# Mixing the filter matrices behind the second image's first chunk

## The chip, the cores and the metric

The kernel runs on one core of one Trainium2 chip. The metric is the device time of one execution in microseconds (us), the median of the runs shown. All data is float32.

## What is computed

Two images of 128 channels and 64 x 64 points go through two layers. The first layer is a group norm, a windowed attention (7 x 7 neighbours, 4 heads) and a small row of linear layers. The second layer treats each image as 4096 tokens of 128 channels:

```python
t = _to_tokens(x)
t = t + _L1_attn_ref(_ln_t(t))          # softmax(q q^T / sqrt(128), diagonal masked) q
t = t + _L1_ffn_ref(_ln_t(t), sigma, phi, M_u, M_phi_plus, M_phi_minus, log_weights, gumbel)
```

The "ffn" is a causal convolution of the tokens with 16 long filters `phi`, each followed by a 128 x 128 matrix, and three short lags with matrices of their own:

```python
out = jnp.einsum('btkd,k,kde->bte', U_plus, s, Mpp)          # s = sigma ** 0.25
out = out + jnp.einsum('btkd,k,kde->bte', U_minus, s, Mpm)
```

There are four such branches, over the whole, the half, the quarter and the eighth of the sequence. They are summed with weights from `log_weights + gumbel`. The kernel uses that the sum over the branches can be taken over the matrices: for each of the 16 filters it mixes the four branches' `M_phi_plus` and `M_phi_minus` by the weights, takes sum and difference, and scales by `s`. This mixing is what the change moves.

## The kernel before, in words

The work runs in this order. First the windowed attention of both images, band by band, in an order that a table of due times (`PLAN`) sets. Then the global attention of image 0 (`attention(0, fill)`, L1233), that of image 1 (L1268), and last the convolution (L1288 and below), where TensorE multiplies spectra (L1320) and applies the mixed matrices (L1332).

`attention` (L882) cuts the 4096 tokens into 8 chunks of 512 and walks over the 36 pairs of chunks. For each pair TensorE makes four score tiles (L899), ScalarE takes their exponentials (L906), and TensorE applies them in both directions: straight (`other`, L952) and, after a transpose (L913) that VectorE copies out of PSUM with a row sum (L916), onto `own` (L927). Pairs on the diagonal have no transposes; on them VectorE adds to the diagonal (L904). The pairs go (0,0), (0,1) ... (0,7), (1,1) ..., so that a chunk is complete at the end of its row.

Between these steps `attention` calls `fill()`. A call asks generators for one more piece of side work each. `filler` (L1191) keeps two lists: `urgent`, which holds one `after` generator (L969) for each finished chunk, and `steps`. Each call goes first to `urgent`, then to `steps`; a generator that yields `None` ends the call, one that yields `True` passes it to the next list. `after` turns a finished chunk back into tokens (L976, L981), takes their layernorm into a tile `z` (L986, L987: statistics L174 and L175, the power on GpSimd L165, the application L182), transposes `z` (L193), transforms it (L1012, L1022) and stores the spectra (L1001, L1030).

Before the change, image 1's `steps` are what image 0 left over (its last `after` generators and the short lags, L1043 to L1060), then `filter_matrices` (L1121), then `load_blocks` (L1259). `filter_matrices` calls `mixed` (L1109), which loads 256 KB at a time into a tile `st` with two buffers (L1114) and sums the four branches on VectorE (L1117, L1119); then come the sum, the difference and the scaling (L1130 to L1135). It fills `mpl` and `mmi`. `load_blocks` fetches the first four blocks of filter spectra `ct` by DMA (L1254). The table `inv` is loaded (L1285) and scaled on VectorE (L1287).

These tiles have no place of their own. The pool `first` holds image 0's normalised tokens `tok[0]` and their transposed copy `cm[0]` (L134, L135), 16 KB each per partition. It is closed at L1237, after image 0's attention is written down, and `mpl`, `mmi`, `inv` and the blocks take its place. So the first write into them has to wait until the last reader of that place is done.

Outside the first attention the order on each engine isn't written by hand: a scheduler orders the instructions at build time by the order in which they were written, the dependencies and its own estimates of durations, and may bring forward one that is free to go. [...] All DMAs named here are issued from SyncE's (SP's) queue.

Of the kernel before, what the change touches and what calls it, by code (L numbers as in the profile page):

```python
# [8 lines left out]
F32 = mybir.dt.float32  # L9
AF = mybir.ActivationFunctionType  # L10
ALU = mybir.AluOpType
# [3 lines left out]
P = 128  # L15
# [6 lines left out]
KF = 16  # L22
# [60 lines left out]
CB, FB, SG = 256, 8, 4  # L83
# [12 lines left out]
def kernel(  # L96
# [16 lines left out]
    nc = tc.nc  # L113
# [4 lines left out]
    first_ = ExitStack()  # L118
# [9 lines left out]
    for c in range(4):  # L128
# [3 lines left out]
    tt, tok, cm = [None, None], [None, None], [None, None]  # L132
# [17 lines left out]
        out=flip, in_=flip, compare_op=ALU.not_equal, fill=1.0, base=1 - QT * QT, pattern=[[0, 2], [1, QT * QT]],  # L150
# [8 lines left out]
    seg = const.tile([P, NBR], F32, name="seg")  # L159
# [26 lines left out]
    def layernorm(dst, src):  # L186

        ln_apply(dst, src, ln_statistics(src))

    def transposed(ps, src):  # L190

        for j in range(src.shape[1]):
            nc.tensor.transpose(ps[:, j * P : (j + 1) * P], src[:, j, :], ident)  # L193
# [30 lines left out]
    with l0a:  # L224
# [6 lines left out]
        sp = l0a.enter_context(tc.tile_pool(name="l0_s", bufs=2))  # L231
# [27 lines left out]
        def table(ci, h, eng):  # L259
# [16 lines left out]
            out=gavg, in_=gavg, compare_op=ALU.is_ge, fill=0.0, base=0,  # L276
# [3 lines left out]
            out=gavg, in_=gavg, compare_op=ALU.is_ge, fill=0.0, base=3,  # L280
# [571 lines left out]
    t_in, t_filter, t_out = _transforms()  # L852
# [5 lines left out]
    with ap_:  # L858
        tp = ap_.enter_context(tc.tile_pool(name="l1_t", bufs=1, side="right"))
        ep = ap_.enter_context(tc.tile_pool(name="l1_e", bufs=8, side="right"))  # L860
        sp = ap_.enter_context(tc.tile_pool(name="l1_s", bufs=2, side="right"))
# [3 lines left out]
        def bank():  # L865
            return ps_m.tile([P, 512], F32, tag="bank", name="bank")
# [15 lines left out]
        def attention(b, fill):  # L882
# [55 lines left out]
            for i, (a, c) in enumerate(pairs):  # L938
# [27 lines left out]
                        nc.vector.tensor_copy(xs, other)  # L966
                es = coming

        def after(b, c, part):  # L969

            n0 = 4 * c
            ph, f0 = divmod(n0, FB)
            par, h = divmod(ph, 2)
            pt = bank()
            for j in range(4):
                nc.tensor.transpose(pt[:, j * P : (j + 1) * P], xa[b][:, (n0 + j) * P : (n0 + j + 1) * P], ident)  # L976
            rden = sp.tile([P, 4], F32, tag="rden", name="rden")
            nc.vector.tensor_reduce(rden, part[:, n0 : n0 + 4, :], AX.X, ALU.add)
            nc.vector.reciprocal(rden, rden)
            for j in range(4):  # L980
                nc.vector.scalar_tensor_tensor(  # L981
                    tt[b][:, n0 + j, :], pt[:, j * P : (j + 1) * P], rden[:, j : j + 1], tt[b][:, n0 + j, :],
                    ALU.mult, ALU.add,
                )
            yield
            z = sp.tile([P, 4, P], F32, tag="z4", name="z4")  # L986
            layernorm(z, tt[b][:, n0 : n0 + 4, :])  # L987
            yield
            yield True
            pt = bank()  # L990
            transposed(pt, z)
            s0 = 1 + h * (TH // 2)
            nc.scalar.copy(
                zc[:, par, s0 : s0 + TH // 2].rearrange("p (c f) -> p f c", f=FB)[:, f0 : f0 + 4, :],
                pt.rearrange("p (f c) -> p f c", f=4),
            )
            yield
            z2 = z.rearrange("p f d -> p (f d)")

            def store(m0, q, src):  # L1000
                nc.sync.dma_start(  # L1001
                    out=us[m0 // 2 : (m0 + P) // 2, :, 2 * h + q, f0 : f0 + 4, b, par, :].rearrange(
                        "g r f d -> (g r) f d"
                    ),
                    in_=src.rearrange("p (f d) -> p f d", d=P),
                )

            for m0 in (0, P):
                for q in range(2):
                    rows_ = slice(q * SB, (q + 1) * SB)  # L1010
                    pu = bank()
                    nc.tensor.matmul(pu, lhsT=tr[rows_, h, m0 : m0 + P], rhs=z2[rows_], start=True, stop=True)  # L1012
                    ub = sp.tile([P, 512], F32, tag="ub", name="ub", bufs=3)
                    (nc.scalar.copy if q else nc.vector.tensor_copy)(ub, pu)
                    store(m0, q, ub)
                yield

            banks = [bank() for q in range(2)]
            for i in range(2):
                for q in range(2):  # L1020
                    rows_ = slice(q * SB, (q + 1) * SB)
                    nc.tensor.matmul(  # L1022
                        banks[q][i * 64 : (i + 1) * 64, 0:256], lhsT=tr[rows_, h, 2 * P : NC],
                        rhs=z2[rows_, i * 256 : (i + 1) * 256], start=True, stop=True,
                    )
            ub = sp.tile([P, 512], F32, tag="ub", name="ub", bufs=3)
            for q in range(2):
                (nc.scalar.copy if q else nc.vector.tensor_copy)(ub[:, q * 256 : (q + 1) * 256], banks[q][:, 0:256])
                for i in range(2):
                    nc.sync.dma_start(  # L1030
                        out=us[P:, :, 2 * h + q, f0 + 2 * i : f0 + 2 * i + 2, b, par, :].rearrange("g r f d -> (g r) f d"),
                        in_=ub[i * 64 : (i + 1) * 64, q * 256 : (q + 1) * 256].rearrange("p (f d) -> p f d", d=P),
                    )
            yield

        def short_lags(b, h):

# [83 lines left out]
        def filter_matrices(mpl, mmi):  # L1121

            for k0 in range(0, KF, 4):
                for dst, src in ((mpl, m_plus), (mmi, m_minus)):
                    mixed(dst[:, k0 : k0 + 4, :], src[:, k0 : k0 + 4])
                    yield

                a, d = (m[:, k0 : k0 + 4, :].rearrange("p k e -> p (k e)") for m in (mpl, mmi))
                s = sp.tile([P, 512], F32, tag="st", name="mdiff")
                nc.vector.tensor_tensor(s, a, d, ALU.subtract)  # L1130
                nc.vector.tensor_tensor(a, a, d, ALU.add)
                for k in range(4):
                    ks = slice(k * P, (k + 1) * P)
                    nc.vector.tensor_scalar(a[:, ks], a[:, ks], sg[:, k0 + k : k0 + k + 1], None, ALU.mult)
                    nc.vector.tensor_scalar(d[:, ks], s[:, ks], sg[:, k0 + k : k0 + k + 1], None, ALU.mult)  # L1135
                yield
# [94 lines left out]
        steps = [drain(), chosen, filters(), tokens(1, bank)]  # L1231
        fill, left = filler(0, steps)
        attention(0, fill)  # L1233
        for gen in steps:
            for _ in gen:
                pass
        first_.close()  # L1237
        l1 = ctx.enter_context(tc.tile_pool(name="l1", bufs=1))
        mpl = l1.tile([P, KF, P], F32, name="mpl")
        mmi = l1.tile([P, KF, P], F32, name="mmi")  # L1240
        inv = l1.tile([P, 3, CB], F32, name="inv")
        ctp = ctx.enter_context(tc.tile_pool(name="blocks", bufs=5))

        def blocks(q):

# [13 lines left out]
        def load_blocks():  # L1259
            for q in range(4):  # L1260
                first_blocks.append(blocks(q))
                yield

        steps = [*left, filter_matrices(mpl, mmi), load_blocks()]

        kept = []
        fill, left = filler(1, steps, kept)
# [13 lines left out]

    tb_ = nc.inline_tensor(t_out, "t_out").ap().rearrange("(a p) c -> p a c", p=P)
    nc.sync.dma_start(out=inv, in_=tb_)  # L1285
    for s, (lo, hi) in enumerate(((0, 32), (32, 64), (64, 128), (128, 256))):
        nc.vector.tensor_scalar(inv[:, :, lo:hi], inv[:, :, lo:hi], seg[:, s : s + 1], None, ALU.mult)  # L1287
    outf = out.rearrange("b c h w -> b c (h w)")  # L1288
    with ExitStack() as cv:
        cp = cv.enter_context(tc.tile_pool(name="conv", bufs=5))  # L1290
# [142 lines left out]
def _transforms():  # L1433


    import numpy as np

    f = np.arange(BINS)[None, :]
    real = (f == 0)

    def parts(n):
        n = np.arange(n)[:, None]
        a = 2 * np.pi * ((f * n) % NC) / NC
        return np.cos(a), -np.sin(a), (1.0 - 2.0 * (n % 2)) + 0.0 * f

    def pack(*cols):
        return np.stack(cols, axis=-1).reshape(cols[0].shape[0], -1).astype(np.float32)

    c, m, alt = parts(CB)
    seg = pack(c, np.where(real, alt, m))  # L1450
    filters = pack(c, np.where(real, 0.0, m), np.where(real, 0.0, -m), np.where(real, alt, c))
    back = np.zeros((3 * P, CB), np.float32)

    back[0:NC] = pack(np.where(real, 1.0, 2.0 * c) / NC, np.where(real, alt, 2.0 * m) / NC).T
    back[NC:] = back[2 * P : NC]
    return seg, filters, back
# [51 lines left out]
```

## Time and profile before

| | us |
|---|---|
| median of 3 runs | 2209.53 (2209.5 to 2211.03) |
| the profiled execution's own time | 2211.93 |
| its span, first to last instruction | 2210.2 |
| TensorE busy (98% of the span) | 2156.2 |
| VectorE busy (42%) | 938.0 |
| ScalarE busy (35%) | 780.6 |
| image 1's attention begins (first score tiles) | 816.9 |
| image 1's first chunk is complete (its L976) | 944.7 |
| image 1's second chunk is complete (its L976) | 1028.2 |

A line of the profile names the engine, the line of the kernel, the operation, the written and read tiles and their shapes. "x2" is the number of instructions in a merged row. A bracket at the end, as in `[1.60 <-DVE z L182]`, says how long the engine had been idle before the row and which instruction released it. PE is TensorE, PEld its weight loads, DVE is VectorE, ACT is ScalarE, POOL is GpSimd, SPq is SyncE's queue, where DMAs are issued.

### The profile page before, as it was taken

The numbers are of one execution on the slowest core, as the hardware profiler recorded it, in microseconds if no ns is written. First come the engines' busy times: TensorE is split into PE (matmuls) and PEld (weight loads), VectorE is DVE, ScalarE is ACT, GpSimd is POOL, SyncE is SP. The second block draws the span as 40 slices with busy tenths as digits, with TensorE's granted clock in tenths as the row PEclk, the third lists the DMA queues.
The fourth block names the chain that finished last, engine by engine and source line by source line (L and its number), as shares of the span: only waits on it lengthen the run. The fifth ranks groups of instructions, "written<-read, shape, count | busy, mean of one in ns | idle before, by whom it ended". The sixth has DMA issues, their size and how long they took to land.

```text
span 2210.2 us, 31763 instructions
## 1 busy us (share of the span) xinstructions
PE 2156.2 (98%) x11920; PEld 1335.0 (60%) x11920; DVE 938.0 (42%) x3054; ACT 780.6 (35%) x1904; POOL 278.5 (13%) x355
## 2 busy tenths in 40 slices
PE   7899998999999998999999999999999999999998
PEld 4677765544554444544544447767767676777776
DVE  5899985434443346433333442232222323232232
ACT  3898883222333222222223232232222323232232
POOL 3477874200000000000000000000000000000000
PEclk8999999999999999999999999999999999999999
DMA  4222212021000025000000141221212121212101
GB/s 147 61 62 61 62 50 52 0 77 43 24 24 25 24 68 156 24 25 24 0 25 24 48 111 40 59 52 47 59 44 55 43 56 43 57 42 57 40 10 77
DMA packets 170345, 110.54 MB, mean 50 GB/s; under 512 B 21311, under 2 KB 155087, under 8 KB 169680
## 3 DMA queue, kind: packets, MB, share of 16 engines
q1 hardware_dynamic: 169266, 105.01, 17.8%
q8 instruction: 94, 1.54, 0.3%
q0 software_dynamic: 576, 2.10, 0.3%
q10 hardware_dynamic: 350, 1.41, 0.3%
q14 instruction: 59, 0.48, 0.1%
HBM read 73.86 MB, written 34.63 MB: 49 GB/s over the span
## 4 chain that ended last, share of the span: by engine, by line
PE 88%; DVE 5%; POOL 3%; DMA 2%; ACT 1%; issue 1%; SPq 1%; POOLq 0%; DVEq 0%; ACTq 0%
PE acc L1332 25%; PE pc L1320 13%; PE own L927 11%; PE bank L899 11%; PE other L952 8%; PE bank L913 4%; PE bank L333 2%; PE bank L1053 2%; PE bank L193 1%; PE bank L543 1%; PE bank L1012 1%; PE py L1354 1%; PE bank L507 1%; DMA st<-in_m_minus_dram 1%; PE po L565 1%; DVE ln_st L379 1%
## 5 line engine op out<-in xcount | busy, mean ns | idle before, releaser
L1321 DVE COPY y<-pc 128x512 f32<-128x512 f32 x320 | 221.6, 692 | 351.5 <-PE pc L1320 347.8
L906 ACT ACTIVATE e<-bank 128x512 f32<-128x512 f32 x288 | 171.8, 597 | 516.2 <-PE bank L899 387.8
L899 PE MATMUL bank<-cm 128*128 128x512 f32 x576 | 297.9, 601 | 1.4 <-DVE y L654 1.4
L1332 PE MATMUL acc<-y,mpl 128*128 128x256 f32 x1280 | 292.1, 382 | 0.0
L1332 PE MATMUL acc<-y,mmi 128*128 128x256 f32 x1280 | 288.0, 379 | 0.0
L1320 PE MATMUL pc<-ct,ut 64*128 64x512 f32 x1280 | 285.2, 595 | 0.9 <-issue 0.9
L1332 PEld LDWEIGHTS acc<-y,mpl 128*128 128x128 f32 x1280 | 238.1, 190 | 59.4 <-issue 29.6
L1332 PEld LDWEIGHTS acc<-y,mmi 128*128 128x128 f32 x1280 | 242.6, 190 | 32.6
L927 PE MATMUL own<-et,tok 128*128 128x512 f32 x448 | 228.5, 597 | 7.5 <-DVE part L916 7.4
L1321 ACT COPY y<-pc 128x512 f32<-128x512 f32 x320 | 205.1, 641 | 86.6 <-PE pc L1320 86.6
L952 PE MATMUL other<-e,tok 128*128 128x512 f32 x448 | 229.7, 594 | 0.0
L1320 PEld LDWEIGHTS pc<-ct,ut 64*128 64x128 f32 x1280 | 121.5, 187 | 145.8 <-issue 140.6
L916 DVE CUSTOM_DVE_ANT_0 et<-bank,one 128x512 f32<-128x512 f32 x224 | 145.5, 687 | 131.5 <-PE bank L913 131.4
L1339 ACT COPY ob<-acc 128x256 f32<-128x256 f32 x32 | 19.0, 595 | 387.0 <-PE acc L1332 387.0
L927 PEld LDWEIGHTS own<-et,tok 128*128 128x128 f32 x448 | 84.4, 191 | 117.5 <-issue 73.3
L952 PEld LDWEIGHTS other<-e,tok 128*128 128x128 f32 x448 | 85.2, 191 | 107.8 <-issue 106.0
L1356 DVE TENSOR_TENSOR xa<-py,xa 128x512 f32<-128x512 f32 x32 | 22.1, 692 | 281.4 <-PE py L1354 281.4
L913 PEld LDWEIGHTS bank<-ident,e 128*128 128x128 f32 x896 | 102.9, 141 | 55.4 <-issue 47.0
L899 PEld LDWEIGHTS bank<-cm 128*128 128x128 f32 x576 | 94.5, 191 | 67.9 <-issue 44.7
L165 POOL TENSOR_TENSOR ln_rs<-ln_rs,mhalf 128x4 f32<-128x4 f32 x24 | 24.5, 1020 | 837.1 <-DVE ln_rs L164 837.1
L530 ACT ACTIVATE p<-p,mn 128x196 f32<-128x196 f32 x256 | 114.4, 449 | 14.3 <-DVE mn L520 13.8
L913 PE MATMUL bank<-ident,e 128*128 128x128 f32 x896 | 117.2, 274 | 0.0
(210 smaller groups left out, 2289.3 us busy)
## 6 DMA issues: line engine op xcount, KB each, us to landing
ut<-us SPq DMA_DIRECT2D x80, 256.0 KB
us<-ub SPq DMA_DIRECT2D x64, 256.0 KB
vw<-vd SPq DMA_DIRECT2D x256, 49.0 KB
ct<-gs SPq DMA_DIRECT2D x160, 72.0 KB
ct<-gs SPq DMA_DIRECT2D x160, 64.0 KB
gs<-sum SPq DMA_DIRECT2D x20, 256.0 KB
vd<-v SPq DMA_DIRECT2D x128, 32.0 KB
st<-in_m_plus_dram SPq DMA_DIRECT2D x16, 256.0 KB
```

The lines of the kernel that those rows point to most:

```text
L333: nc.tensor.matmul(pl, lhsT=wg[:, lo : lo + P], rhs=zT, start=True, stop=True)
L530: nc.scalar.activation(p, p, AF.Exp, bias=t[name + "mn"][:, h : h + 1], scale=-1.0, accum_out=t["den"][:, u, h : h + 1],)
L899: nc.tensor.matmul(ps, lhsT=cm[b][:, n * P : (n + 1) * P], rhs=cm[b][:, chunk(c)], start=True, stop=True)
L906: nc.scalar.activation(e, ps, AF.Exp, bias=0.0, scale=ASCALE, accum_out=part[:, n, c : c + 1])
L913: nc.tensor.transpose(pt[:, k * P : (k + 1) * P], es[k][:, m * P : (m + 1) * P], ident)
L916: nc.vector.tensor_tensor_reduce(et, pt, one, 1.0, 0.0, ALU.mult, ALU.add, part[:, n, a : a + 1])
L927: nc.tensor.matmul(own, lhsT=tok[b][:, n, :], rhs=e, start=first, stop=last)
L952: nc.tensor.matmul(other, lhsT=tok[b][:, 4 * CHUNKS[a] + j, :], rhs=es[j], start=(j == 0), stop=(j == 3))
L1053: nc.tensor.matmul(py, lhsT=mu[:, lag, :], rhs=zc[:, from_par, s0 : s0 + 512], start=(lag == 0), stop=(lag == 2))
L1320: nc.tensor.matmul(pc, lhsT=ut[fp, b, par, :], rhs=cv_[fp], start=True, stop=True)
L1321: (nc.scalar.copy if f else nc.vector.tensor_copy)(y[:, 4 * f : 4 * f + 4, :, par, b * 2 * FB + q : (b + 1) * 2 * FB : 2], pc.rearrange("p ...
L1332: nc.tensor.matmul(acc, lhsT=(mmi if l else mpl)[:, k, :], rhs=y[:, 1::2, k, ::-1, :] if l else y[:, 0::2, k, :, :], start=(l == 0 and k = ...
```

## The change

`filter_matrices`, the load and scaling of `inv` and `load_blocks` become one generator, `for_ffn`. It stands where the two generators stood in image 1's `steps`. As long as a flag isn't set it yields `True` and does nothing. The flag is the list `spare`: it starts with a slice of image 0's token tile, `tok[0][:, 0:4, :]`. The first `after` of image 1 takes that slice as its `z` in place of a tile of its own, and when it is at its end it puts `None` into the list. Only then does `for_ffn` close the pool `first`, open the pools behind it and begin the mixing. No instruction of the mixing is added or removed.

```diff
+        spare = [tok[0][:, 0:4, :]]
+
         def after(b, c, part):
...
-            z = sp.tile([P, 4, P], F32, tag="z4", name="z4")
+            borrowed = b == 1 and spare not in ([], [None])
+            z = spare.pop() if borrowed else sp.tile([P, 4, P], F32, tag="z4", name="z4")
             layernorm(z, tt[b][:, n0 : n0 + 4, :])
...
             yield
+
+            if borrowed:
+                spare.append(None)
...
-        first_.close()
-        l1 = ctx.enter_context(tc.tile_pool(name="l1", bufs=1))
-        mpl = l1.tile([P, KF, P], F32, name="mpl")
-        mmi = l1.tile([P, KF, P], F32, name="mmi")
-        inv = l1.tile([P, 3, CB], F32, name="inv")
-        ctp = ctx.enter_context(tc.tile_pool(name="blocks", bufs=5))
+        mpl, mmi, inv, ctp = [None] * 4
...
-        steps = [*left, filter_matrices(mpl, mmi), load_blocks()]
+        def for_ffn():
+
+            nonlocal mpl, mmi, inv, ctp
+            while spare != [None]:
+                yield True
+            first_.close()
+            l1 = ctx.enter_context(tc.tile_pool(name="l1", bufs=1))
+            mpl = l1.tile([P, KF, P], F32, name="mpl")
+            mmi = l1.tile([P, KF, P], F32, name="mmi")
+            inv = l1.tile([P, 3, CB], F32, name="inv")
+            ctp = ctx.enter_context(tc.tile_pool(name="blocks", bufs=5))
+            yield from filter_matrices(mpl, mmi)
+
+            nc.sync.dma_start(out=inv, in_=nc.inline_tensor(t_out, "t_out").ap().rearrange("(a p) c -> p a c", p=P))
+            for s, (lo, hi) in enumerate(((0, 32), (32, 64), (64, 128), (128, 256))):
+                nc.vector.tensor_scalar(inv[:, :, lo:hi], inv[:, :, lo:hi], seg[:, s : s + 1], None, ALU.mult)
+            yield
+            yield from load_blocks()
+
+        steps = [*left, for_ffn()]
...
-    tb_ = nc.inline_tensor(t_out, "t_out").ap().rearrange("(a p) c -> p a c", p=P)
-    nc.sync.dma_start(out=inv, in_=tb_)
-    for s, (lo, hi) in enumerate(((0, 32), (32, 64), (64, 128), (128, 256))):
-        nc.vector.tensor_scalar(inv[:, :, lo:hi], inv[:, :, lo:hi], seg[:, s : s + 1], None, ALU.mult)
```

## The prediction

> **What bounds the kernel now.** I read the page's engine line first, then TensorE's (PE's) waits by stretches of 200 us, then the table of stretches around the only place where PE waits for work of the change, and last the orders of PE and VectorE (DVE) in it. The page and the waits of PE from 800 to 1300 us (us in total, times, longest):
>
> ```profile
> PE 2156.2 (98%) x11920; PEld 1335.0 (60%) x11920; DVE 938.0 (42%) x3054; ACT 780.6 (35%) x1904; POOL 278.5 (13%) x355
> PE own L927 <- DVE part L916: 6.5, 5, 4.4
> PE bank L193 <- DVE z L182: 5.1, 3, 1.9
> PE own L927 <- DVE xa L931: 1.6, 2, 0.8
> ```
>
> PE is the bound nearly everywhere. A change that adds and removes no matmul can only win or lose PE's idle time and its slow clock. Both sit in one place. The table (stretch, its length, busy us of PE, PEld, DVE, ACT, POOL; granted clock; DMA share; GB/s):
>
> ```profile
> 816.00:830.00 14.00, 13.19 (x42) 5.19 (x43) 7.30 (x16) 6.62 (x18) 0.28 (x1) 1.00 0.72 194
> 830.00:850.00 20.00, 15.58 (x44) 7.13 (x42) 13.94 (x44) 4.63 (x12) 1.30 (x1) 0.83 0.60 165
> 850.00:900.00 50.00, 48.46 (x167) 23.45 (x166) 34.67 (x82) 11.47 (x29) 0.00 (x0) 1.00 0.44 127
> 900.00:940.00 40.00, 40.00 (x134) 20.55 (x133) 12.06 (x34) 8.95 (x26) 0.00 (x0) 1.00 0.00 0
> 980.00:1020.00 40.00, 40.00 (x136) 20.76 (x136) 12.38 (x36) 8.95 (x26) 0.00 (x0) 1.00 0.00 1
> ```
>
> The second image's attention starts at 816. The mixing (L1117 to L1135) runs from 817 to 897, and PE idles there; from 900 on it doesn't idle at all. PE in order of time, then DVE just before PE's long wait:
>
> ```profile
> 836.48 1.02 PE L952 MATMUL other<-e,tok 128*128 128x512 f32 x2
> 841.93 2.07 PE L927 MATMUL own<-et,tok 128*128 128x512 f32 x2 [4.42 <-DVE part L916]
> 843.79 1.06 PE L193 MATMUL bank<-ident,z 128*128 128x128 f32 x4
> 844.65 1.91 PE L899 MATMUL bank<-cm 128*128 128x512 f32 x2
> 846.35 1.78 PE L952 MATMUL other<-e,tok 128*128 128x512 f32 x2
> 847.97 1.02 PE L927 MATMUL own<-et,tok 128*128 128x512 f32 x2
> ```
>
> ```profile
> 831.77 1.60 DVE L1119 SCALAR_TENSOR_TENSOR mmi<-st,wt,mmi 128x512 f32<-128x512 f32 x2 [3.23 <-DMA st<-in_m_minus_dram]
> 833.40 0.69 DVE L1130 TENSOR_TENSOR mdiff<-mpl,mmi 128x512 f32<-128x512 f32 x1
> 836.05 1.12 DVE L981 SCALAR_TENSOR_TENSOR tt<-bank,rden,tt 128x128 f32<-128x128 f32 x4
> 840.15 1.11 DVE L182 TENSOR_SCALAR z<-tt,ln_mv,ln_rs 128x128 f32<-128x128 f32 x4 [0.90 <-POOL ln_rs L165]
> 841.18 0.68 DVE L916 CUSTOM_DVE_ANT_0 et<-bank,one 128x512 f32<-128x512 f32 x1
> ```
>
> DVE waits 3.23 us for a load of the mixing, does a mixing group, then the layernorm chain of the first image's last chunk (L981 to L182, whose matmuls at L976 were done by 831.5), and only then the copy L916 that PE wants at 837.5. Chain and mixing meet: that is the stall. After it PE runs at half speed until 847.97.
>
> [...] 4.42 us idle, then rows twice as long for 6.0 us, clock 0.83 in that stretch. The 1.59 us wait at 816 brought no such rows. [...]
>
> **The change part by part.**
> *The old place is cleared.* (a) The wait of 4.42 us goes. (b) The slow clock goes: from 841.93 to 847.97 is 6.04 us; the same rows at full speed take 0.86 + 0.43 + 0.86 + 0.86 = 3.0 (steps of undisturbed rows: 0.86 per two 512-wide matmuls, 0.43 per four transposes); 3.0 us. (c) The 850 to 900 stretch idles 50.00 - 48.46 = 1.5 us. Together 9.0 us. What stays late there is the chain alone with L916: free of mixing it starts at 831.5, takes about 5 us (836.05 to 841.2), and L916 follows in time for 837.5; I book 0.3. The waits at the end of the first image's attention don't belong to the mixing: at the second image's end, with none near, they are 0.35, 0.78 and 1.60 us again. They stay.
>
> *The new place.* The mixing's first write needs the token space free. The borrowed slice is last read by L1022 of the second image's first chunk, at 959.3 to 960.0. So the work begins at about 960. The list:
> - DVE: 24 L1119 x 0.75 = 18.0, 8 L1117 x 0.48 = 3.8, 8 of L1130 and L1131 x 0.69 = 5.5, 32 of L1134 and L1135 at 0.20 a step = 6.4, and inv's four (0.47 + 0.35 + 0.48) = 1.3: 35.0 us.
> - SP: 32 loads of 256 KB into two buffers, 16 block loads (64 and 72 KB) and inv's. Each st issue takes 0.37 us. Two st loads go out early, as they do before (at 358 us). A late load takes 2.8 us to the DVE that waits for it (issued 883.3, used 886.1). The block loads come off SP while the first st loads wait, so the first waits will be the long ones again. On SP the stores of the next chunk (1035 to 1044) may queue behind an st load that waits for its buffer; three ub buffers and ACT's slack cover it; nothing booked.
> - POOL and PE get nothing; the yields only shift who is asked next. The borrowed slice itself costs nothing: the token space was last read at 815, and z is written at 949.
> DVE there carries 12.38 / 40 = 31% of its own. With 35 us of mixing and about 20 us of waits for st (11.3 + 9.0 before), T = 0.31 T + 55 gives 80 us: it runs from 960 to about 1040, as long as before. DVE then has no slack, and what is queued behind each waiting L1119 is L916, with PE's L927 behind that. L916 has about 1 us of cover (it may start when L913 ends; PE asks 1.7 us later, after L899 and L952; one L916 takes 0.69).
>
> Unknown, bounded: PE's loss in these 80 us. Nearest row: 850 to 900, mixing in the same manner without the long collision, 1.5 us in 47 us of mixing, so 2.5 us in 80. Below: 0, if all waits fall in the cover; a gain below nothing is excluded, since PE idles nowhere from 900 to 1200. Above: 9 us or more, the old place over again. I take 2.5.
>
> Second unknown: the tail meets the layernorm chain of the second chunk (L981 at 1028.87 to z at 1033.6), and PE's transposes of z come at 1033.82, 0.2 us later. A delay of z by a wait plus an op would show at once. In its favour: no L916 stands between 1024.8 and 1039.9, for that pair is diagonal. From 0 to 7.4 us (wait and clock as in a and b); I take 1.0.
>
> Sum: -9.0 + 0.3 + 2.5 + 1.0 = -5.2 us. The profiled execution took 2211.93 us for a span of 2210.2; it would take 2206.7. The runs' median is 2209.53, 2.4 lower; the same step gives 2204.3.
>
> **The rivals.** 0.2% is about what a measurement of this kernel can tell from no change: below 2205.1 is faster, above 2213.9 slower.
> - *Everything hidden*: new losses under 2 us. For it: a pair of chunks leaves DVE 8 of 12 us free, and no chain lies in most of the stretch. Against: the 0.55 and 0.85 us waits of 861 and 881, where the chain was already gone. About 2209.5 - 9.0 + 1.0 = 2201.5.
> - *The stall moves along*: the tail hits the chain at 1029[...]. 7.4 in place of the 1.0 above: 2209.5 - 9.0 + 0.3 + 2.5 + 7.4 = 2210.7. For it: the overlap in time. Against: the diagonal pair.
> - *Slower, a saturated DVE*: the work is now asked for directly before each pair's L916, where before it was written behind the first image's leftovers, so groups of ten ops (3 us) and waits may stand ahead of L916 each time. 80 us hold 13 bursts of two L916. If each makes PE wait, the change loses from 9 / 13 = 0.7 us a burst on; at 0.8 us, with two slow-clock spells of 3.0, it is -9.0 + 0.3 + 10.4 + 6.0: 2217. Against: 850 to 900 shows two waits of more than half a us in seven bursts.
> - *The change doesn't do what it says*, the mixing staying at 817: excluded as far as the code goes, since its place is freed only after the borrowed slice.
>
> **How the numbers follow.** Forecast (new losses of 2 to 6 us, 2202.5 to 2206.8): 0.50. Hidden: 0.18. Stall moved along: 0.22. Slower: 0.10. Faster by over 0.2%: all of hidden and 0.36 of the forecast's 0.50 (the part below 2205.1), 0.54. Slower: 0.10, and 0.01 of the moved stall. Within: 0.35. The range reaches from hidden's 2200.3 (nearly no loss at all) to 2211.5, just over the moved stall; what is left out is the slower case, some 0.1, and edges of the others, under 0.1.
>
> **What would show it.** Right: no L1117 or L1119 between 816 and 955; no wait of over 1 us by PE from 817 to 900 and no clock below 1.00; the second image's first L976 some 8.5 us earlier than 944.7; mixing about 80 us long; PE waits for L916 of 0.2 to 1 us in it. Wrong: [...] waits at every burst; or losses at 830 to 900 that stay although the mixing has gone, which would put them on the chain alone.

## The result and the profile after

| | before | after |
|---|---|---|
| median of 22 runs each | 2210.38 | 2207.82 |
| ratio, 95% interval | | 0.9984 (0.9979 to 0.9990) |
| profiled execution's own time | 2211.93 | 2204.96 |
| its span | 2210.2 | 2203.3 |

By the ratio the change makes the kernel faster by 0.16%, some 3.5 us; the medians lie 2.6 us apart. That is the way that was forecast, by half to two thirds of the forecast 5.2 us, and inside the 0.2% called no change. The range holds it.

The page's engine line, and TensorE's waits from 800 to 1300 us, after:

```profile
PE 2152.5 (98%) x11920; PEld 1333.0 (61%) x11920; DVE 936.9 (43%) x3054; ACT 779.5 (35%) x1904; POOL 277.7 (13%) x355
PE bank L193 <- DVE z L182: 5.1, 3, 1.9
PE own L927 <- DVE part L916: 4.7, 7, 1.2
PE own L927 <- DVE xa L931: 1.6, 2, 0.8
```

The wait of 4.4 us is gone; there are more waits for L916, and the longest is 1.2. The table of stretches, after:

```profile
816.00:830.00 14.00, 14.00 (x46) 5.47 (x46) 3.49 (x10) 7.62 (x20) 0.00 (x0) 1.00 0.30 86
830.00:850.00 20.00, 20.00 (x78) 9.51 (x77) 8.90 (x30) 6.58 (x16) 1.01 (x1) 1.00 0.20 59
850.00:900.00 50.00, 50.00 (x166) 25.67 (x165) 12.95 (x33) 11.28 (x30) 0.00 (x0) 1.00 0.03 6
980.00:1000.00 20.00, 17.70 (x59) 8.69 (x58) 13.12 (x32) 3.53 (x11) 0.00 (x0) 1.00 0.41 119
1000.00:1020.00 20.00, 18.62 (x61) 8.90 (x59) 16.24 (x41) 3.91 (x12) 0.00 (x0) 1.00 0.36 105
```

The old place is clean: no idle time, full clock. Idle time is back between 980 and 1020, 3.7 us in these two rows. TensorE (first fence) and VectorE (second) in order of time, at one of the new waits:

```profile
982.65 1.02 PE L952 MATMUL other<-e,tok 128*128 128x512 f32 x2
984.89 1.13 PE L927 MATMUL own<-et,tok 128*128 128x512 f32 x2 [1.22 <-DVE part L916]
985.85 1.02 PE L899 MATMUL bank<-cm 128*128 128x512 f32 x2
```

```profile
982.02 0.75 DVE L1126 SCALAR_TENSOR_TENSOR mmi<-st,wt,mmi 128x512 f32<-128x512 f32 x1 [1.42 <-DMA st<-in_m_minus_dram]
982.81 0.69 DVE L1137 TENSOR_TENSOR mdiff<-mpl,mmi 128x512 f32<-128x512 f32 x1
983.53 0.69 DVE L1138 TENSOR_TENSOR mpl<-mpl,mmi 128x512 f32<-128x512 f32 x1
984.14 0.68 DVE L916 CUSTOM_DVE_ANT_0 et<-bank,one 128x512 f32<-128x512 f32 x1
```

(L1126, L1137 and L1138 are the lines 1119, 1130 and 1131 of before.) The transposes that L916 reads (L913, begun at 980.91) were done by 982. VectorE was then still waiting for a load, and had three operations of the mixing to do before L916.

How much was really lost can be measured better than by idle times. The order of TensorE's instructions in the two kernels is the same but for one exchanged pair, so each matmul can be matched with itself in another run and timed against fixed points: A, the transposes of z (L193) that follow the 1.6 us wait at the end of image 0's attention; the completion of image 1's first and second chunk (L976, L979 after); and B, that same L193 at the end of image 1's attention. Differences in us; the last row is a kernel of the experiments without the mixing, and the last column compares the whole way from A to B with it:

| kernel | A | A to 1st chunk | 1st to 2nd | 2nd to B | loss by the mixing |
|---|---|---|---|---|---|
| before | 816.81 | 127.92 | 83.50 | 241.28 | 10.6 |
| after | 814.60 | 117.34 | 89.23 | 241.42 | 5.9 |
| after, profiled again | 815.83 | 117.34 | 92.01 | 241.42 | 8.6 |
| no mixing (e3) | 816.20 | 117.34 | 83.50 | 241.29 | 0 |

The first column is the noise of the stages before: the profiled execution of after was 2.2 us ahead before any of the change ran (and was the fastest of its 22). The rest repeats to 0.01 us where the mixing isn't.

### The profile page after: what moved, and what is told of

The parts are those of the page before. It is cut to its first block, busy times and chain, and to the rows that moved or that the text cites. A ratio compares the mean times of both kernels' runs of the same rounds, so it can differ in the third digit from the quotient of the medians.

```text
span 2203.3 us, 31767 instructions
## 1 busy us (share of the span) xinstructions
PE 2152.5 (98%) x11920; PEld 1333.0 (61%) x11920; DVE 936.9 (43%) x3054; ACT 779.5 (35%) x1904; POOL 277.7 (13%) x355
## 4 chain that ended last, share of the span: by engine, by line
PE 88%; DVE 5%; POOL 3%; DMA 2%; ACT 1%; issue 1%; SPq 0%; POOLq 0%; DVEq 0%; ACTq 0%
PE acc L1349 25%; PE pc L1337 13%; PE bank L899 10%; PE own L927 10%; PE other L952 8%; PE bank L913 4%; PE bank L333 2%; PE bank L1060 2%; PE bank L193 2%; PE bank L543 2%; PE bank L1016 2%; PE py L1371 1%; PE bank L507 1%; PE po L565 1%; DMA st<-in_m_plus_dram 1%; POOL ln_rs L387 1%
## 5 line engine op out<-in xcount | busy, mean ns | idle before, releaser
L916 DVE CUSTOM_DVE_ANT_0 et<-bank,one 128x512 f32<-128x512 f32 x224 | 145.9, 686 | 110.9 <-PE bank L913 110.7
L913 PEld LDWEIGHTS bank<-ident,e 128*128 128x128 f32 x896 | 102.9, 141 | 55.4 <-issue 47.2
L165 POOL TENSOR_TENSOR ln_rs<-ln_rs,mhalf 128x4 f32<-128x4 f32 x24 | 24.2, 1006 | 832.7 <-DVE ln_rs L164 832.7
L913 PE MATMUL bank<-ident,e 128*128 128x128 f32 x896 | 117.2, 274 | 0.0
```

What stands on the lines that cost most here:

```text
L913: nc.tensor.transpose(pt[:, k * P : (k + 1) * P], es[k][:, m * P : (m + 1) * P], ident)
L916: nc.vector.tensor_tensor_reduce(et, pt, one, 1.0, 0.0, ALU.mult, ALU.add, part[:, n, a : a + 1])
```

## The experiments

All ratios are to the kernel before, with 95% intervals. "Stretch 1" is A to the first chunk (floor 117.34), "stretch 2" from the first to the second chunk (floor 83.50).

**The changed kernel again (e1).** No edit.

> The changed kernel once more, for a second profile of it. Theory A (VectorE stands behind loads of the mixing, and TensorE behind VectorE; before, this met the layernorm chain and the slow clock): TensorE idles 3 to 5 us between 940 and 1040 as in the first profile (4.0 us), no slow clock, ratio to before 0.9984. Rival B (the first profile was a lucky one, in typical runs the new place loses more): 6 us or more of idle time there, with a clock below 1.00.

Measured: 0.9987 (0.9981 to 0.9994). Stretch 2 took 92.01, 2.8 us more than in the first profile. TensorE's longer waits in it:

```profile
987.46 1.12 PE L927 MATMUL own<-et,tok 128*128 128x512 f32 x2 [1.99 <-DVE part L916]
1001.06 1.12 PE L927 MATMUL own<-et,tok 128*128 128x512 f32 x2 [1.28 <-DVE part L916]
1020.99 1.98 PE L927 MATMUL own<-et,tok 128*128 128x512 f32 x4 [1.70 <-DVE part L916]
```

These three stand at the same matmuls as in the first profile, each longer; the clock stays at 1.00. All waits there sum to 6.4 us against 4.0. Rival B is right in its first half (6 us or more of idle time, so the first profile was a lucky one) and wrong in its second, the slow clock. VectorE's waits for loads in the two summed to 18.2 and 21.1 us.

**Without the gate (e2).**

```diff
-        spare = [tok[0][:, 0:4, :]]
+        spare = [None]
...
-            while spare != [None]:
-                yield True
```

> The change without its gate: the generator doesn't wait for the flag and no slice is borrowed, so the mixing falls back to the old place, while the joined generator and the earlier inv stay. Theory A: the place alone matters, so the time of before, ratio 0.999 to 1.001, and the long wait of 4 us with the slow clock is back near 840. Rival C (the joining or the earlier inv brings part of the gain): ratio 0.9985 or less.

Measured: 0.9997 (0.9988 to 1.0005), stretch 1 at 128.2, a wait of 4.32 us and the slow rows behind it, as theory A had it. The joining and the earlier inv bring nothing that can be measured; the gain hangs on the gate.

**Without the mixing (e3).**

```diff
-                    mixed(dst[:, k0 : k0 + 4, :], src[:, k0 : k0 + 4])
+                    nc.sync.dma_start(out=dst[:, k0 : k0 + 4, :], in_=src[0, k0 : k0 + 4].rearrange("k d e -> d k e"))
                     yield
-                a, d = (m[:, k0 : k0 + 4, :].rearrange("p k e -> p (k e)") for m in (mpl, mmi))
...
```

> The changed kernel without the mixing: branch 0's matrices are loaded straight into place by 8 loads, all VectorE work of the mixing and 24 of 32 loads are left out. Theory A: what is left is the floor of any place for the mixing, TensorE idles under 0.5 us from 816 to 1040, 9.0 us under before, ratio 0.9959, and 4 us under the changed kernel. Rival D (part of the loss near 840 is the layernorm chain's own, not the mixing's): idle time or slow clock stays near 840 and the ratio stays above 0.997.

Measured: 0.9950 (0.9937 to 0.9962). Stretch 1 takes the same 117.34 as in the changed kernel: the chain alone costs nothing there, rival D falls, and the change takes all that can be had in the old place. By times the mixing cost 0.0050 x 2210 = 11 us before, and (0.9984 - 0.9950) x 2210 = 7.5 us after (8.2 with e1's ratio; e3's interval alone makes it uncertain by some 3 us).

**Six buffers (e4).** In `mixed`, the tile for a load takes turns in three tags that are free by then.

```diff
-                st = sp.tile([P, 4, P], F32, tag="st", name="st")
                 n = src.shape[1]
+                tag = ("st", "sum", "ph")[len(turn) % 3] if n == 4 else "st"
+                turn.append(tag)
+                st = sp.tile([P, 4, P], F32, tag=tag, name="st")
```

> The changed kernel with six buffers for the mixing's loads in place of two (it takes turns in the places of two tiles that are free by then); same VectorE work, same place. Theory A: VectorE's waits for these loads fall from some 18 us to under 6, TensorE's idle time in the stretch from 4.0 to under 1.5 us, ratio to before 0.996 to 0.9975. Rival E (VectorE's ops themselves, in groups of ten, delay the copies out of PSUM, not the waits): idle time stays at 3 us or more, ratio 0.998.

Measured: 0.9965 (0.9953 to 0.9978), better than the change, but with stretch 2 at 87.7 still 4.2 us over its floor. VectorE's waits fell to 3.3 us in all; two of them (1.44 and 1.31 us), each right after the eight scalings that end a group, made TensorE wait 1.93 and 1.48. Theory A's ratio came, its idle time of under 1.5 us didn't. Here waits and operations add up: neither theory A nor rival E alone.

**Two loads (e6), no groups (e7).** They take the two apart. In e6, `mixed` loads its first two tiles and reads them again after that; in e7 the lines for sum, difference and scaling are gone.

```diff
...
+                if n == 4 and len(held_) == 2:
+                    st = held_[i % 2]
+                else:
+                    st = sp.tile([P, 4, P], F32, tag="st" if n < 4 else "sum", name="st")
+                    nc.sync.dma_start(out=st[:, 0:n], in_=src[i].rearrange("k d e -> d k e"))
+                    if n == 4:
+                        held_.append(st)
```

> The changed kernel with 2 of the mixing's 32 loads: the two tiles are read again and again, 30 loads are left out, all of VectorE's operations stay. From first to second chunk it takes 83.5 us without the mixing, 89.2 and 92.0 in two profiles of the changed kernel, 87.7 with six buffers. Theory A (waits for loads): 84 to 85.5 us, ratio to before 0.9950 to 0.9960. Rival E (the ops in groups ahead of the copy): 87 us or more, ratio 0.9965 or above.

> The changed kernel with the four groups of sum, difference and scaling left out (40 operations, 12 us of VectorE); all loads and the summing over branches stay. Theory A: the waits for loads stay and with them most of the loss, 87 us or more from first to second chunk (83.5 without mixing), ratio 0.9970 to 0.9985. Rival E: 85.5 us or less, ratio under 0.9965.

Measured: e6 0.9954 (0.9941 to 0.9966), stretch 2 at 84.2; e7 0.9971 (0.9961 to 0.9981), stretch 2 at 89.6. In the new place all of the mixing's operations, without waits, cost 0.7 us; the waits, with two thirds of VectorE's mixing time left, cost 6.1. The waits for loads are the cause. Whether the groups make it worse is not shown: 6.1 lies within the changed kernel's 5.9 and 8.6, and by times e7's interval touches that of the change.

**The old place without the waits (e5, e9).** e5 is the kernel before with the six buffers of e4, e9 the kernel before with the two loads of e6.

> The kernel before with six buffers for the mixing's loads in place of two, the mixing in its old place. Without the mixing the stretch from the second image's start to its first chunk takes 117.3 us, before it takes 127.9. Theory A (VectorE's wait for a load is what makes the collision): the 4.4 us wait falls under 3 us, no slow clock, 119 to 122 us in the stretch, ratio 0.9965 to 0.998: six buffers alone do as much as the move or more. Rival F (the old place is bad in itself, mixing ops and layernorm chain together): 126 us or more, ratio 0.999 or above.

> The kernel before with 2 of the mixing's 32 loads, 30 loads left out, all of VectorE's operations of the mixing in the old place. To the first chunk: 117.3 us without the mixing, 127.9 before, 126.7 with six buffers. Theory A' (it needs the waits for loads, and the few that six buffers left were enough to hold up the chain): 117.5 to 120 us, ratio 0.9950 to 0.9965. Rival F (operations and chain alone collide in the old place): 123 us or more, ratio 0.998 or above.

Measured: e5 0.9997 (0.9991 to 1.0004), stretch 1 at 126.7; e9 0.9975 (0.9967 to 0.9984), 122.4. Both of my expectations were missed: e5 fell where rival F had put it, e9 between the two. VectorE's waits for loads in e5 are down to 6.4 us from 21.9, and the loss is nearly whole. TensorE and VectorE in e5:

```profile
839.08 0.45 PE L193 MATMUL bank<-ident,z 128*128 128x128 f32 x1 [4.50 <-DVE z L182]
840.36 2.08 PE L927 MATMUL own<-et,tok 128*128 128x512 f32 x2 [0.84 <-DVE part L916]
```

```profile
831.91 0.75 DVE L1123 SCALAR_TENSOR_TENSOR mpl<-st,wt,mpl 128x512 f32<-128x512 f32 x1 [1.30 <-DMA st<-in_m_plus_dram]
832.58 1.12 DVE L981 SCALAR_TENSOR_TENSOR tt<-bank,rden,tt 128x128 f32<-128x128 f32 x4
836.47 0.48 DVE L1121 TENSOR_SCALAR mpl<-st,wt 128x512 f32<-128x512 f32 x1 [1.05 <-DMA st<-in_m_plus_dram]
838.58 1.11 DVE L182 TENSOR_SCALAR z<-tt,ln_mv,ln_rs 128x128 f32<-128x128 f32 x4 [0.90 <-POOL ln_rs L165]
```

The layernorm chain starts late behind mixing operations and a wait, has three more mixing operations and a wait of 1.05 us inside it, and TensorE waits 4.5 us for its end, and behind it the slow rows are back (the matmuls at 840.36 take 2.08 us, not 1.02). In e9 there is no wait for loads at all, and 5.1 us are lost. TensorE, ScalarE and SP's queue:

```profile
832.65 1.13 PE L899 MATMUL bank<-cm 128*128 128x512 f32 x2 [1.78 <-ACT ub L1014]
839.82 0.33 PE L193 MATMUL bank<-ident,z 128*128 128x128 f32 x1 [0.88 <-DVE z L182]
841.20 1.12 PE L927 MATMUL own<-et,tok 128*128 128x512 f32 x2 [1.05 <-DVE part L916]
```

```profile
832.01 0.58 ACT L1014 COPY ub<-bank 128x512 f32<-128x512 f32 x1 [7.19 <-issue]
```

```profile
814.67 10.19 SPq L1261 DMA_DIRECT2D ct<-gs  x16
824.90 0.59 SPq L1292 DMA_DIRECT2D inv<-t_out  x1
825.59 0.98 SPq L1001 DMA_DIRECT2D us<-ub  x2
```

Matched matmul by matmul with e3, 2.4 us are the chain and the copy behind mixing operations, and 0.6 a copy at 857. The 1.78 us wait, 2.1 us lost, is new: the pool's closing frees the filter blocks' place too, and their first 16 loads hold SP for 10.2 us. The chunk's stores come behind them. The first is issued 9.4 us after A, against 7.6 in the changed kernel, where no such load stands there. ScalarE's copy L1014, which needs a free ub tile, starts 6.4 us after that issue (825.59 to 832.01), ScalarE having idled for 7.19, and TensorE waits for ScalarE; the load of inv and four more block loads go out around that store. In the changed kernel the same copy starts 2.4 us after the store's issue (822.19 to 824.61), and there the profile names the store as what it waited for (1.39 us). So of the delay, 5.8 us, less than a third (1.8) is SP's queue, and the rest lies between the store's issue and the copy. That it is a slow landing of the store is my reading: in e9 the profile names nothing that ended the wait. In before the same block loads go out in turns with the mixing's, and there, matched with e3, TensorE loses nothing up to its long wait at 841.93. So what the gate takes away from one layernorm chain in before is the waits and the operations; the block loads cost TensorE something of their own only where they go out in one row.

**On GpSimd (e8).** The mixing in the old place, each VectorE operation of it on GpSimd (`nc.vector` to `nc.gpsimd`, the multiply-add as two operations).

> The kernel before with the whole mixing on GpSimd, which is idle there: scaling in place and adding are two operations instead of one, by rows of the profile 32 x 1.5 + 24 x 1.3 + 8 x 1.3 + 32 x 0.8 = some 115 us, from 817 to 932 and so between two chunks. VectorE then waits for no load. Theory A: 117.5 to 119.5 us to the first chunk, near the floor, ratio 0.9950 to 0.9962, the best of all. Against it: the power of the layernorm chain at 838 stands behind GpSimd's waits for loads and operations of 1.5 us, and may make TensorE wait 2 to 4 us for z[...]: then 122 us or more, ratio 0.998.

Measured: 1.0015 (1.0008 to 1.0022), slower. After 848 TensorE waits nowhere up to the end of the attention, but before that it waits 4.15 us for z at 817, and then (TensorE, then GpSimd):

```profile
847.95 2.08 PE L927 MATMUL own<-et,tok 128*128 128x512 f32 x2 [8.50 <-DVE part L916]
```

```profile
843.13 1.57 POOL L1118 TENSOR_SCALAR mpl<-st,wt 128x512 f32<-128x512 f32 x1
844.66 1.05 POOL L165 TENSOR_TENSOR ln_rs<-ln_rs,mhalf 128x4 f32<-128x4 f32 x1
```

The chain's power L165 was ready at 835.9 and stands behind a whole group on GpSimd until 844.7; z and the copy L916 behind it come late. The expectation had named this as what spoke against it, at 2 to 4 us. The price moved to another queue and rose.

**Spread out (e10, e11).** The changed kernel, with one mixing operation for each call of `fill` (two additions, or four scalings, together in the groups), each queued on VectorE behind the latest L916 written down by then. That edge sets the order only. e10 has six buffers for the loads, e11 the two of the changed kernel. In both the difference (`mdiff`) no longer takes one of the loads' buffers, as it does in the changed kernel.

```diff
-                nc.vector.tensor_tensor_reduce(
+                behind[:] = [nc.vector.tensor_tensor_reduce(
...
+                with tc.issue_after(behind[0].ins):
                     if i == 0:
                         nc.vector.tensor_scalar(dst2, st2, wt[:, 0:1], None, ALU.mult)
                     else:
                         nc.vector.scalar_tensor_tensor(dst2, st2, wt[:, i : i + 1], dst2, ALU.mult, ALU.add)
+                yield
...
-                s = sp.tile([P, 512], F32, tag="st", name="mdiff")
+                s = sp.tile([P, 512], F32, tag="z4", name="mdiff")
```

> The changed kernel with six buffers, and the mixing spread: one operation of VectorE (or two in the scaling) for each piece of side work, each queued behind the latest copy out of PSUM at that point, in place of four to ten in a row. Same loads and operations, about 130 us long instead of 75. Theory A (a load that isn't there when VectorE comes to it, with a copy queued behind): every load is there in time, 83.5 to 84.5 us from first to second chunk and no loss after, ratio 0.9950 to 0.9960, as without the mixing. Rival E' (a copy that comes late by one operation of 0.75 us already costs): 2 us or more are lost in all, ratio 0.9965 or above.

> The same spreading with the two buffers of the changed kernel. Theory A: with one load per 3 us and 2.8 us from issue to use, most loads are in time; waits of VectorE for them under 6 us in all, a loss of 0.5 to 2 us, ratio 0.9952 to 0.9968. If the depth of buffering and not the pace is what counts, the loss stays at 4 us or more, ratio 0.9970 or above.

Measured: both 0.9950 (0.9936 to 0.9963, and 0.9937 to 0.9962), medians 2199.42 and 2199.75, both stretches on their floors. The whole mixing is hidden, with two buffers. The buffer that `mdiff` gave up isn't enough to explain it: e7 has no `mdiff` and two buffers, and lost 6.1 us. VectorE in e11 (L918 is the copy, L1142 the mixing):

```profile
965.53 0.69 DVE L918 CUSTOM_DVE_ANT_0 et<-bank,one 128x512 f32<-128x512 f32 x1 [0.60 <-PE bank L915]
...
966.76 1.54 DVE L1142 SCALAR_TENSOR_TENSOR mmi<-st,wt,mmi 128x512 f32<-128x512 f32 x2
971.56 0.69 DVE L918 CUSTOM_DVE_ANT_0 et<-bank,one 128x512 f32<-128x512 f32 x1 [3.26 <-PE bank L915]
```

The mixing goes into the gap behind each pair of copies, its loads are there, and the next copy finds VectorE idle for 3.26 us. It takes 166 us (950.7 to 1116.6) in place of 75, and over all of it VectorE waits 0.4 us for loads. Against the changed kernel that is another 0.9950 / 0.9984 = 0.9966.

**Spread out, no gate (e12).** The same edit on the kernel before.

> The kernel before (no gate, no borrowed slice, two buffers) with the spreading of the run before: one mixing operation for each piece of side work, each queued behind the latest copy out of PSUM. The mixing then follows the first image's leftovers in the order of the code, and runs on over the first chunk's layernorm chain. Theory A (how closely the operations are packed ahead of their loads decides, not the place): no loss, 117.3 to 118 us to the first chunk, 83.5 to 84 to the second, ratio 0.9950 to 0.9962. Rival F (the place must be clear of a layernorm chain): 2 us or more are lost at the chain, ratio 0.9965 or above.

Measured: 0.9952 (0.9939 to 0.9966), stretch 1 at 118.4, stretch 2 at 83.5. The mixing runs from 887 to 1050, so it too has left the old place, and it runs over the first chunk's layernorm chain, which costs nothing. The 1.1 us in stretch 1 come before it begins: TensorE waits 0.76 us at 829.9 for ScalarE, which waits for its ub tile, with the same 16 block loads ahead on SP as in e9 (10.2 us) and a copy that starts 5.4 us after the store's issue (823.82 to 829.27). That is what the gate is still worth in this profile once the mixing is spread; by the times it can't be told from nothing (0.9952 against 0.9950).

## Why the prediction came out as it did

*The old place, -9.0 and +0.3: right in mechanism, too small.* It gave -10.6 (127.92 to 117.34). The +0.3 for the chain alone was 0 (e3). The -9.0 missed 1.6 because I took idle time for loss, and a late matmul costs more. At 881.24 of before the bracket says 0.85; the step from the row before it was 1.87 instead of 0.86, and the step after it 0.96 instead of 0.86, so 1.11 were lost. Rows also overlap: undisturbed ones of 1.02 us busy time begin 0.86 apart. Some rows are late without any bracket, TensorE before:

```profile
867.68 1.12 PE L952 MATMUL other<-e,tok 128*128 128x512 f32 x2
868.95 1.13 PE L927 MATMUL own<-et,tok 128*128 128x512 f32 x2
```

From 867.68 to 868.95 are 1.27 in place of 0.86. Matched with e3, the long wait and the slow clock cost 7.6 (4.42 + 3.0 predicted), and 850 to 900 cost 3.0, where I had read 1.5.

*The new place, +2.5: the step that failed.* It was 5.7 and 8.5 us in two profiled executions; by the times all of the mixing cost 7.5. The length was right (predicted 80 us, measured 75, from 947.7 to 1022.4), and so was the cause (e6, e7). The rate was wrong: I took 1.5 us in 47 from 850 to 900, two waits, and scaled it by length. Those 1.5 us of idle time were 3.0 us of loss; scaled in the same way they give about 5 us for 80 (an estimate), near the first profile's 5.7. So the same misreading accounts for the larger part. What remains goes with where a wait for a load falls against a copy, five times in the first profile and six or seven in the second; it differs from one execution to the next. I had named a reason for more (the work is now written directly before each pair's L916) and gave it only to the slower rival; no run tests it alone. With the measured 7.5 the sum would have been -3.1.

*The tail and the chain, +1.0: not there.* The mixing ended at 1022.4, just as the second chunk's chain began (L984 at 1022.36), and what follows lost 0.1 us (241.42 against 241.28). The mixing was some 5 us shorter than predicted, so the overlap that the term was for didn't come about.

*SP, nothing booked: right for this change, and in part by luck.* I looked at the stores in the new place, where nothing showed, and not at the block loads that leave the old one. In before they cost TensorE nothing of their own; sent out in one row they cost 2.1 us in e9 and 1.1 in e12. Whether they made the mixing's own loads slower in before is not shown.

*The starting point.* The profiled execution would have taken 2206.7 by my sum; it took 2204.96, with 2.2 us of it from the stages before A. The sum over its own stretches is -4.7. That the forecast came near is in part luck: the old place gave 1.9 more than booked and the new one cost some 4 more (7.5 by the times, against 3.5), two errors, largely of one origin, that pull in opposite directions. A slip besides: the forecast's lower end, 2202.5, leaves out the 0.3 for the chain that its upper end has.

*The rivals.* "Everything hidden" has no run in this change, but e10 and e11 show that it can be had. "The stall moves along" didn't come: no idle time over 2 us, and the clock at 1.00 from 816 to 1250 in both profiles. "Slower" needed 0.7 us for each of 13 bursts; it was 5.7 to 8.5 in all, 0.4 to 0.65 a burst; the 7.5 by the times is closer to its turning point of 9 than to my 2.5. "Doesn't do what it says" is out: the first operation of the mixing stands at 947.7. The slow clock came again in e2, e5 and e8: rows about twice as long (2.08 us in place of 1.02) after idle times of 4.32, 4.50, 4.15 and 8.50 us. At what idle time it begins is not shown: behind the 1.60 us wait at the end of image 1's attention the clock was 0.50 from 1272 to 1274 in before and from 1265 to 1267 in after, and 1.00 from 1250 to 1300 in e1 and e2. (So the slow clock of before sat in two places; the second stands behind B, in both kernels.) How long it lasts is not settled either: the slow rows went on for 6.0 us in before and for some 3 us after the 8.50 us wait in e8. That VectorE held back a copy behind a load it doesn't need shows after the change too: 1.42 us at 982.02, then three operations of the mixing, then L916.

What stays open: how long the loads take from one execution to the next, and why; two profiles show the spread, no run varies it alone. In e10 and e11 two things were changed together, one operation at a time and the order behind L916; no run has one without the other.

## What to carry to other kernels

Work that fills an idle engine isn't hidden because the engine has time. Here it was hidden where its inputs were there when the engine came to it, since an operation that waited held up the copy behind it (1.42 us at 982.02 in after), and where no urgent chain stood behind a row of it: in e9 such operations, without any wait for a load, cost 2.4 us in the old place. Ordering each such operation behind the last urgent one, one at a time, made 35 us of VectorE work and 8 MB of loads free with two buffers, where deeper buffers, another place and another engine did not. When a step moves, count its DMA issues where it leaves as well as where it joins, and the time from a store's issue to the work that needs its tile (6.4 us in e9, 2.4 in after). And read a loss from the steps between matched matmuls: idle times showed half of it from 850 to 900.

## What the runs showed that I had not expected

- From 800 us on, TensorE's rows took about twice as long after idle times of 4.15 us (e8, at 817), 4.32 (e2), 4.42 (before), 4.50 (e5) and 8.50 us (e8), and not after one of 1.99 (e1). After the 1.60 us at the end of image 1's attention the clock fell to 0.50 for some 3 us in before and after, and not in e1 and e2.
- GpSimd took 1.57 us for a scaling and 1.27 us for an addition of 128 x 512, VectorE 0.48 and 0.69.
- 16 block loads of 64 and 72 KB held SP's queue for 10.2 us, 0.64 us each (e9), and the copy that needs the tile of the first store behind them started 6.4 us after its issue, where without them it starts 2.4 after it.
